# Slot numbers carried in a node's row, and adjacency degrees split between the table and the blocks, in a four-layer graph kernel

## The chip, the cores and the metric

The kernel runs on one core of a Trainium2 chip. The metric is the device time of one execution in microseconds, as the median of several. The record marks each execution as fast or slow by its time and clock; all that are told of here are fast. Engines are called as in the profile: PE (matmuls), PEld (weight loads, beside PE), DVE, ACT, POOL, SP.

## The reference, cut to what matters

Four layers, each `x = layernorm(x + layer(x, adj))`, with x of 8 x 2048 x 64 and a dense 2048 x 2048 adjacency `adj`. Only the first layer is touched. It mixes each node with its hyperedges (64 of them, mask `H` of 2048 x 64, 1 to 12 a node):

```python
h = x @ W
alpha = softmax(where(H.T > 0, leaky_relu(h @ a_node), NEG))        # over nodes
agg = einsum('ben,bnf->bef', alpha, h)                              # one row a hyperedge: the "table"
beta = sigmoid((h @ a_gn)[:, None, :] + (agg @ a_ge)[:, :, None])
all_he = elu(beta * h + (1 - beta) * agg)                           # per node and hyperedge: the "blocks"
coefs1 = softmax(where(H > 0, attn(elu(agg)), NEG))                 # over a node's hyperedges
g = einsum('bne,benf->bnf', coefs1, all_he)
deg = maximum(adj.sum(-1), 1)
industry = einsum('nm,bmf->bnf', adj / deg, x @ W_ind)              # the "products"
```

## The kernel before

Nodes are sorted by their number of hyperedges (`order`). A row tile is 128 sorted nodes; it needs as many blocks as its fullest node has hyperedges: 12, 5, 5, 4, 4, 4, 3, 3, 3, 3, 2, 2, 2, 2, 2, 1, together 57. Block s of a tile takes each node's s-th hyperedge. A **slot number** (0, or 1 to 12) says for each pair of hyperedge and node which block that is. A **one-hot** is the 128 x 128 matrix `slot == s + 1`; a matmul with it picks table rows.

Before, the rows of H are gathered in sorted order, and the slot numbers of all 2048 nodes lie ready in one resident tile `slot` before the first block:

```python
for t in range(NT):
    nc.gpsimd.indirect_dma_start(out=hs[:, t, :], in_=h_ne, in_offset=...order[:, t:t + 1]...)
...
for c in range(NCH):      # masks, transposes, cumulative count
    ...
    nc.vector.tensor_tensor(slot[:, cols(c)], pcm, mt, ALU.mult)
```

The block stage interleaves blocks with the product matmuls, which `fill(n)` hands out:

```python
def begin(t):
    hrow = pl.tile([P, BF + 8], F32, tag="hrow", bufs=2)
    nc.gpsimd.indirect_dma_start(out=hrow, in_=hs_hbm[:], ...order[:, t:t + 1]...)    # row fetch
    S = sum(n > t for n in SLOT_TILES)
    both = split(pb, hrow[:, 0:BF], "hr", 2, [P, BF])
    for s in range(S):
        o = pl.tile([P, P], F32R, tag="o", bufs=17)
        nc.gpsimd.tensor_scalar(o, slot[:, cols(t, P)], float(s + 1), None, op0=ALU.is_equal)
        mm(ps[:, s]..., lhsT=o, rhs=ts2, start=True, stop=True)                       # one-hot sums
    ...                                                                               # R, co on DVE
now = begin(0)
for t in range(NT):
    S, both, ohs, R, co = now
    for s in range(S):
        for i, (l, r) in enumerate(((ident_r, both[0]), (ident_r, both[1]), (ohs[s], tab2))):
            mm(pz, lhsT=l, rhs=r, start=i == 0, stop=i == 2)
        if s == 0 and t + 1 < NT:
            fill(3)
            now = begin(t + 1)
        fill(8)
        ...                                 # pz *= R (DVE), y = exp (ACT), elu and * co (DVE)
        nc.gpsimd.tensor_tensor(acc, acc, y, ALU.add)
```

Each engine runs its instructions in the order that the scheduler gave it. Products work on x split into a high half (a cast on ACT) and a low half (a subtraction, here on DVE).

## Time and profile before

The median of three runs is 2227.4 us (2225.26 to 2234.32). From the profiled execution:

| point of the first layer | us |
|---|---|
| first row fetch for the blocks | 101.31 |
| first product matmul | 112.2 |
| last product matmul ends | 292.84 |
| first gather of the next layer | 297.5 |
| span | 2227.2 |

Read it as two stages: up to 112 us the table and the adjacency, bound by loads; from there the blocks, bound by PE. The views are in the prediction. This is the timeline (start, length, engine, line, operation, count of instructions; in brackets the engine's idle time before it and what ended it; `...` marks lines left out):

```profile
163.59 1.24 POOL L623 TENSOR_SCALAR o<-slot 128x128 fp32r<-128x128 bf16 x2
166.66 0.53 POOL L623 TENSOR_SCALAR o<-slot 128x128 fp32r<-128x128 bf16 x1 [1.83 <-PE pz L171]
...
172.18 0.51 PE L171 MATMUL ps<-ts,o 128*128 128x16 f32 x4
```

POOL makes one-hots in small groups between other work and, in this view, is held only by `pz`, that is, by an old one-hot's buffer that a block still reads. When PE comes to the sums it does four in 0.51 us.

### The profile page before, as it was taken

The numbers are of one execution on the slowest core, as the hardware profiler recorded it, in microseconds if no ns is written. First come the engines' busy times: TensorE is split into PE (matmuls) and PEld (weight loads), VectorE is DVE, ScalarE is ACT, GpSimd is POOL, SyncE is SP. The second block draws the span as 40 slices with busy tenths as digits, with TensorE's granted clock in tenths as the row PEclk, the third lists the DMA queues.
The fourth block names the chain that finished last, engine by engine and source line by source line (L and its number), as shares of the span: only waits on it lengthen the run. The fifth ranks groups of instructions, "written<-read, shape, count | busy, mean of one in ns | idle before, by whom it ended". The sixth has DMA issues, their size and how long they took to land.

```text
span 2227.2 us, 19810 instructions
## 1 busy us (share of the span) xinstructions
PE 1993.1 (89%) x7318; PEld 1289.3 (58%) x7318; DVE 1139.1 (51%) x1900; ACT 338.3 (15%) x584; POOL 551.0 (25%) x499
## 2 busy tenths in 40 slices
PE   7799978888759999799999999999986989999994
PEld 4488745555644444375456456447434777777873
DVE  5479956666532222216864773782784344331312
ACT  1322323222111111010010001001000011111110
POOL 5457466564323323200110110110010001010202
PEclk7889989999969999999999999999998999999997
DMA  8723334322210000000000000000001223200000
GB/s 263 237 66 91 95 91 107 83 70 63 76 46 0 19 19 19 19 24 5 10 5 3 10 8 1 10 8 3 8 8 32 76 72 85 62 19 1 20 1 21
DMA packets 99306, 103.26 MB, mean 46 GB/s; under 512 B 63088, under 2 KB 63136, under 8 KB 99008
## 3 DMA queue, kind: packets, MB, share of 16 engines
q1 hardware_dynamic: 73248, 83.09, 12.8%
q0 software_dynamic: 4064, 9.10, 1.7%
q10 hardware_dynamic: 21888, 9.70, 1.6%
q8 instruction: 60, 0.98, 0.2%
q14 instruction: 46, 0.38, 0.1%
HBM read 75.59 MB, written 26.28 MB: 46 GB/s over the span
## 4 chain that ended last, share of the span: by engine, by line
PE 63%; DVE 12%; DMA 12%; POOL 7%; issue 4%; ACT 2%; SPq 0%; ACTq 0%; POOLq 0%; DVEq 0%
PE py L967 18%; PE u L171 17%; PE u L914 10%; PE u L527 9%; DMA fcav<-in_adj_t 7%; POOL ln_r L155 3%; PE pz L171 2%; DVE fcav L1061 2%; PE pf L171 1%; PE pr L171 1%; DMA x<-x_hbm 1%; DVE ln_v L151 1%; DVE ln_c L145 1%; DVE ln_m L143 1%; ACT r L149 1%
## 5 line engine op out<-in xcount | busy, mean ns | idle before, releaser
L967 PE MATMUL py<-wp,xg 128*128 128x512 f32 x1024 | 448.5, 597 | 8.5 <-DVE fcav L972 5.8
L967 PEld LDWEIGHTS py<-wp,xg 128*128 128x128 f32 x1024 | 193.6, 191 | 254.4 <-issue 216.4
L171 PE MATMUL u<-adj,hi 128*128 128x512 f32 x768 | 256.5, 415 | 0.0
L171 PE MATMUL u<-adj,lo 128*128 128x512 f32 x768 | 246.5, 400 | 1.1 <-DVE lo L1026 1.1
L914 PE MATMUL u<-pt,xn 128*128 128x512 f32 x512 | 227.5, 603 | 8.3 <-DVE u L923 7.1
L972 DVE TENSOR_TENSOR fcav<-py,emb_n 128x512 f32<-128x512 f32 x256 | 177.0, 691 | 52.0 <-PE py L967 37.5
L975 POOL TENSOR_TENSOR r<-r,bias 128x256 f32<-128x256 f32 x32 | 23.3, 729 | 636.0 <-DVE r L973 636.0
L973 DVE TENSOR_REDUCE r<-fcav 128x32 f32<-128x512 f32 x256 | 175.4, 685 | 8.1
L914 PEld LDWEIGHTS u<-pt,xn 128*128 128x128 f32 x512 | 97.3, 193 | 130.2 <-issue 114.7
L527 PE MATMUL u<-adj,vh 128*128 128x512 f32 x512 | 158.3, 408 | 15.4 <-ACT vh L166 11.6
L171 PEld LDWEIGHTS u<-adj,hi 128*128 128x128 f32 x768 | 143.2, 190 | 40.8 <-issue 11.5
L171 PEld LDWEIGHTS u<-adj,lo 128*128 128x128 f32 x768 | 144.6, 190 | 35.4 <-DVE lo L1026 1.6
L527 PE MATMUL u<-adj,vl 128*128 128x512 f32 x512 | 152.1, 398 | 0.0
L155 POOL TENSOR_TENSOR ln_r<-ln_e,neg_half 128x8 f32<-128x8 f32 x64 | 106.1, 1658 | 174.9 <-DVE ln_e L153 166.9
L908 DVE TENSOR_SCALAR pt<-pt 128x512 f32<-128x512 f32 x64 | 49.1, 784 | 172.8 <-ACT pt L907 171.3
L1045 POOL TENSOR_TENSOR r<-r,xn 128x512 f32<-128x512 f32 x16 | 20.4, 1275 | 418.9 <-DVE r L1044 418.9
L527 PEld LDWEIGHTS u<-adj,vh 128*128 128x128 f32 x512 | 96.2, 189 | 45.7 <-ACT vh L166 13.1
L912 POOL TENSOR_TENSOR acc<-acc,pt 128x512 f32<-128x512 f32 x60 | 79.6, 1327 | 162.6 <-DVE pt L908 159.8
L527 PEld LDWEIGHTS u<-adj,vl 128*128 128x128 f32 x512 | 96.4, 189 | 22.1 <-issue 0.7
L1061 DVE SCALAR_TENSOR_TENSOR fcav<-fcav,adj 128x512 f32<-128x512 f32 x64 | 44.5, 695 | 117.6 <-DMA fcav<-in_adj_t 117.1
L149 ACT ACTIVATE r<-ln_c 128x512 f32<-128x512 f32 x64 | 40.4, 631 | 288.4 <-DVE ln_c L145 274.8
L709 POOL DMA_INDIRECT gn<-gs_hbm,rank x64 | 69.7, 1088 | 34.7 <-issue 14.2
(316 smaller groups left out, 2774.3 us busy)
## 6 DMA issues: line engine op xcount, KB each, us to landing
a<-in_adj_t SPq DMA_DIRECT2D x32, 512.0 KB, 5.9
fcav<-in_adj_t SPq DMA_DIRECT2D x64, 256.0 KB, 2.8
x_hbm<-r SPq DMA_DIRECT2D x20, 256.0 KB, 2.3
hs_hbm<-st ACTq DMA_DIRECT2D x16, 260.0 KB, 5.4
xt<-in_x_t SPq DMA_DIRECT2D x16, 256.0 KB, 5.4
u_hbm<-ut SPq DMA_DIRECT2D x16, 256.0 KB, 2.7
gs_hbm<-acc SPq DMA_DIRECT2D x16, 256.0 KB, 2.0
ut<-u_hbm SPq DMA_DIRECT2D x16, 256.0 KB, 3.2
```

What stands on the lines that cost most here:

```text
L149: nc.scalar.activation(r, xc, AF.Square)
L155: nc.gpsimd.tensor_tensor(rstd, vare, neg_half[:, :groups], ALU.pow)
L171: tc.keep_in_program_order(nc.tensor.matmul(*args, **kw))
L527: nc.tensor.matmul(u[c], lhsT=half[:, j, :], rhs=adj[t][:, cols(c)], start=t == 0 and i == 0, stop=ends and not own,)
L709: nc.gpsimd.indirect_dma_start(out=gn[:, j, :], out_offset=None, in_=g_rows, in_offset=bass.IndirectOffsetOnAxis(ap=rank4[:, p, c * JT + j ...
L908: nc.vector.tensor_scalar(pt, pt, 1.0, None, op0=ALU.max)
L912: nc.gpsimd.tensor_tensor(acc, acc, pt, ALU.add)
L914: nc.tensor.matmul(u[p], lhsT=xn[p][:, t, :], rhs=pt, start=t == 0, stop=t == NT - 1)
L967: nc.tensor.matmul(py.rearrange("p o d -> p (o d)"), lhsT=xg[b][:, q, cols(j, P)], rhs=wp[:, q, cols(k)], start=q == 0, stop=q == 1,)
L972: nc.vector.tensor_tensor(pr, py, e_b, ALU.mult)
L973: nc.vector.tensor_reduce(r[:, j, b, cols(k, OH)], pr, AX.X, ALU.add)
L1061: nc.vector.scalar_tensor_tensor(a, a, 1.0, adj[t][:, cols(k)].bitcast(F32), op0=ALU.mult, op1=ALU.not_equal, accum_out=left[:, t, k:k + 1],)
```

## The change

Its intent: the 16 gathers of H rows go. Slot numbers are made in natural node order, before `order` is known, and written into the row of each node in HBM, so that the row fetch brings them along. Four of the 16 adjacency tiles, and the degree sums over them, move behind the first row fetch, into the block stage, so that the blocks can begin earlier. Cut to its core:

```diff
-    slot = hy.tile([P, N], BF16, name="slot")
+    HROW = BF + 8 + 2 * E
+    hs_hbm = dram.tile([N, HROW], F32, name="hs_hbm")
...
+        for t in range(NT):
+            nc.tensor.matmul(pcm[:, t, :], lhsT=mt[:, cols(t, P)], rhs=tri_e, start=True, stop=True)
+        nc.vector.tensor_tensor(slot, pcm, m_n, ALU.mult)
+        for i in range(2):
+            queued(nc.sync.dma_start(hs_hbm[:, k:k + E]..., slot))
...
-            st = pa.tile([P, BF + 8], F32, tag="st", name="st", bufs=2)
+            st = pa.tile([P, BF + 8], F32, tag="st", name="st", bufs=3)
...
-                part[c] = split(pb, xc.pop((p, c)), f"v{c}", 1, [P, JT, P])
+                part[c] = split(pb, xc.pop((p, c)), f"v{c}", 1, [P, JT, P], nc.gpsimd)
...
+        def load_adj_end(t):
+            for c in range(NCH):
+                a = pb.tile([P, JT, P], F32, tag="x", name="a", bufs=XB)...
+                nc.sync.dma_start(a, adj_t[t * P:(t + 1) * P, cols(c)])
+                tc.keep_in_program_order(nc.gpsimd.tensor_copy(adj[t][:, cols(c)], a))
...
         def begin(t):
+            fetch_rows(t + 1)
+            hrow = hrows.pop(t)
             S = sum(n > t for n in SLOT_TILES)
+            pt = pps.tile([P, P], F32, tag="mm", name="pslot", bufs=3)
+            transpose(pt, hrow[:, BF + 8:])
+            slot = pl.tile([P, P], BF16, tag="slot", name="slot", bufs=2)
+            nc.scalar.copy(slot, pt)
...
-                nc.gpsimd.tensor_scalar(o, slot[:, cols(t, P)], float(s + 1), None, op0=ALU.is_equal)
+                tc.keep_in_program_order(
+                    nc.gpsimd.tensor_scalar(o, slot, float(s + 1), None, op0=ALU.is_equal)
+                )
...
+        fetch_rows(0)
+        fetch_rows(1)
+        load_adj_end(NT - 4)
+        load_adj_end(NT - 3)
         now = begin(0)
+        load_adj_end(NT - 2)
+        load_adj_end(NT - 1)
...
-                fill(8)
+                fill(7)
```

More of the change, by code (lines that the diff above doesn't have):

```diff
@@ L63, in tile_gnn_fast @@
     adj_t: bass.AP,
-    h_ne: bass.AP,
+    h_en: bass.AP,
+    h_nt: bass.AP,
     w0: bass.AP,
@@ L88, in tile_gnn_fast @@
     B, N, F = x.shape
-    E = h_ne.shape[1]
+    E = h_en.shape[0]
     D = emb.shape[1]
@@ L160, in grouped, with split @@
         return a.rearrange("p t (b f) -> p (t b) f", f=F)
-    def split(pool, src, tag, bufs, shape):
+    def split(pool, src, tag, bufs, shape, eng=nc.vector):
         hi = pool.tile(shape, F32R, tag=f"{tag}h", name=f"{tag}h", bufs=bufs)
@@ L166, in split @@
         nc.scalar.copy(hi, src)
-        nc.vector.tensor_tensor(lo, src, hi, ALU.subtract)
+        eng.tensor_tensor(lo, src, hi.bitcast(F32) if eng is nc.gpsimd else hi, ALU.subtract)
         return hi, lo
@@ L201, in tile_gnn_fast @@
     order = hy.tile([P, NT], U32, name="order")
-    slot = hy.tile([P, N], BF16, name="slot")
     inv_row = hy.tile([P, N], F32, name="inv_row")
-    tri2 = hy.tile([P, P], BF16, name="tri2")
-    nc.vector.memset(tri2, 0.0)
-    make_upper_triangular(nc, tri2[0:E, 0:E], 1.0, diag=True)
-    nc.vector.tensor_copy(tri2[E:P, E:P], tri2[0:E, 0:E])
-    hs_hbm = dram.tile([N, BF + 8], F32, name="hs_hbm")
+    HROW = BF + 8 + 2 * E
+    hs_hbm = dram.tile([N, HROW], F32, name="hs_hbm")
     x1_hbm = [dram.tile([P, NT, P], F32, name=f"x1_hbm{p}") for p in range(NP)]
@@ L219, in tile_gnn_fast @@
     adj = [adj_pool.tile([P, N], F32R, name=f"adj{t}") for t in range(NT - XT)]
+    ph_scope = ExitStack()
+    pph = ph_scope.enter_context(tc.tile_pool(name="ph", bufs=1, space=PSUM))
     with tc.tile_pool(name="pa", bufs=1) as pa, tc.tile_pool(name="pa_ps", bufs=1, space=PSUM) as pps:
@@ L227, in tile_gnn_fast @@
         m_n = pa.tile([P, NT, E], F32, name="m_n")
-        nc.sync.dma_start(m_n, h_ne.rearrange("(t p) e -> p t e", p=P))
+        nc.sync.dma_start(m_n, h_nt)
+        m_en = pa.tile([E, N], F32, name="m_en")
+        nc.scalar.dma_start(m_en, h_en)
         xt = [xs.tile([P, NP, P], F32, name=f"xt{t}") for t in range(NT)]
@@ L242, in tile_gnn_fast, with queued @@
             nc.scalar.dma_start(bd66[b * F:(b + 1) * F, b, 0:F], w0)
+        def queued(dma):
+            tc.keep_in_program_order(dma)
         def load_adj(t):
@@ L248, in load_adj @@
                 a = pa.tile([P, HN], F32, tag="a", name="a", bufs=4)
-                nc.sync.dma_start(a, adj_t[t * P:(t + 1) * P, cols(k, HN)])
-                if t < NT - XT:
-                    nc.gpsimd.tensor_copy(adj[t][:, cols(k, HN)], a)
-                else:
-                    nc.scalar.copy(adj[t][:, cols(k, HN)], a)
-        for t in range(NT - XT):
+                queued(nc.sync.dma_start(a, adj_t[t * P:(t + 1) * P, cols(k, HN)]))
+                nc.gpsimd.tensor_copy(adj[t][:, cols(k, HN)], a)
+        for t in range(4):
             load_adj(t)
@@ L314, in tile_gnn_fast @@
         nc.vector.tensor_scalar(wrong[:, 1:2], pc[:, 0:1], float(N), None, op0=ALU.is_lt)
+        tri_e = pa.tile([E, E], BF16, name="tri_e")
+        make_upper_triangular(nc, tri_e, 1.0, diag=True)
+        mt = pa.tile([E, N], BF16, name="mt")
+        nc.vector.tensor_scalar(mt, m_en, 0.0, None, op0=ALU.is_gt)
+        pcm = pph.tile([P, 2, C], F32, tag="ph", name="pcm", bufs=2)
+        pcm = pcm.rearrange("p k (t e) -> p (k t) e", e=E)
+        for t in range(NT):
+            nc.tensor.matmul(pcm[:, t, :], lhsT=mt[:, cols(t, P)], rhs=tri_e, start=True, stop=True)
+        slot = pa.tile([P, NT, E], F32, name="slot")
+        nc.vector.tensor_tensor(slot, pcm, m_n, ALU.mult)
+        for i in range(2):
+            k = BF + 8 + i * E
+            queued(nc.sync.dma_start(hs_hbm[:, k:k + E].rearrange("(t p) e -> p t e", p=P), slot))
+        for t in range(4, NT - XT):
+            load_adj(t)
         tl = pa.tile([P, NT], F32, name="tl")
@@ L346, in tile_gnn_fast @@
         nc.vector.scalar_tensor_tensor(order, po[:, 0, :], float(P), olo, op0=ALU.mult, op1=ALU.add)
-        hs = pa.tile([P, NT, E], F32, name="hs")
-        for t in range(NT):
-            nc.gpsimd.indirect_dma_start(
-                out=hs[:, t, :], out_offset=None, in_=h_ne,
-                in_offset=bass.IndirectOffsetOnAxis(ap=order[:, t:t + 1], axis=0),
-            )
         for dst, v in ((fcb_col, fc_b), (av_col, av)):
@@ L374, in tile_gnn_fast @@
         for t in range(NT):
-            ph = pps.tile([P, 2, C], F32, tag="ph", name="ph", bufs=2)
+            ph = pph.tile([P, 2, C], F32, tag="ph", name="ph", bufs=2)
             for p in range(NP):
@@ L402, in tile_gnn_fast @@
             )
-            nc.scalar.dma_start(hs_hbm[t * P:(t + 1) * P, :], st)
+            nc.scalar.dma_start(hs_hbm[t * P:(t + 1) * P, 0:BF + 8], st)
             for k in range(2):
@@ L414, in tile_gnn_fast, with degrees @@
         adj_end = ctx.enter_context(tc.tile_pool(name="adj_end", bufs=1, side="right"))
-        for t in range(NT - XT, NT):
-            adj.append(adj_end.tile([P, N], F32R, name=f"adj{t}"))
-            load_adj(t)
-        du = [pps.tile([P, 2, C], F32, tag="ph", name=f"du{g}", bufs=2) for g in range(2)]
-        ones_r = pa.tile([P, P], F32R, name="ones_r")
+        adj += [adj_end.tile([P, N], F32R, name=f"adj{t}") for t in range(NT - XT, NT)]
+        ones_r = hy.tile([P, P], F32R, name="ones_r")
         nc.gpsimd.tensor_copy(ones_r, ones)
-        def degrees(first, end):
-            for t in range(first, end):
+        du = [pph.tile([P, 2, C], F32, tag="ph", name=f"du{g}", bufs=2) for g in range(2)]
+        def degrees():
+            for t in range(NT):
                 for c in range(NCH):
@@ L430, in degrees, with some_degrees @@
                     )
-        degrees(0, 8)
-        for c in range(NCH):
-            m2 = pa.tile([P, JT, 2, E], F32, tag="m2", name="m2", bufs=2)
-            for i in range(2):
-                nc.vector.tensor_scalar(m2[:, :, i, :], hs[:, c * JT:(c + 1) * JT, :], 0.0, None, op0=ALU.is_gt)
-            pt = pps.tile([P, C], F32, tag="sm", name="pt", bufs=2)
-            for j in range(JT):
-                nc.tensor.transpose(pt[:, cols(j, P)], m2[:, j].rearrange("p i e -> p (i e)"), ident)
-            mt = pa.tile([P, C], BF16, tag="mt", name="mt", bufs=2)
-            nc.scalar.copy(mt, pt)
-            pcm = pps.tile([P, C], F32, tag="sm", name="pcm", bufs=2)
-            nc.tensor.matmul(pcm, lhsT=tri2, rhs=mt, start=True, stop=True)
-            nc.vector.tensor_tensor(slot[:, cols(c)], pcm, mt, ALU.mult)
+                    yield
+        degree_passes = degrees()
+        def some_degrees(tiles):
+            for _ in range(tiles * NCH):
+                next(degree_passes)
+        some_degrees(6)
         gv = pagg[:, :, 0:G * (F + 1)].rearrange("p k (g c) -> p k g c", c=F + 1)
@@ L458, in tile_gnn_fast @@
         )
-        tab = pa.tile([E, B, F], F32, tag="st", name="tab", bufs=2)
+        tab = pa.tile([E, B, F], F32, tag="st", name="tab", bufs=3)
         tsm = pa.tile([E, 2, B], F32, name="tsm")
@@ L480, in tile_gnn_fast @@
             ))
-        degrees(8, 10)
+        some_degrees(2)
         het = pa.tile([P, NP, E], F32, name="het")
@@ L488, in tile_gnn_fast @@
             nc.scalar.activation(tf[:, b], pf, AF.Tanh, bias=fcb_col)
-        degrees(10, NT - XT)
+        some_degrees(2)
         pse = pps.tile([E, B], F32, tag="sm", name="pse", bufs=2)
@@ L493, in tile_gnn_fast @@
                 mm(pse[:, 2 * p + b:2 * p + b + 1], lhsT=tf[:, b, p, :], rhs=av_col, start=True, stop=True)
-        degrees(NT - XT, NT)
         nc.vector.tensor_scalar(sc[:, 1, :], pse, CLIP, -CLIP, op0=ALU.min, op1=ALU.max)
@@ L503, in tile_gnn_fast @@
         nc.vector.tensor_tensor(ts2[E:P, :], tsf, ts2[0:E, :], ALU.subtract)
-        for g in range(2):
-            nc.scalar.copy(inv_row[:, cols(g, 2 * C)], du[g].rearrange("p k c -> p (k c)"))
     def load_x(dst, p, c):
@@ L542, in tile_gnn_fast @@
         pps = pb_scope.enter_context(tc.tile_pool(name="pb_ps", bufs=1, space=PSUM))
+        XB = 5
         def products():
@@ L547, in fetch @@
             def fetch(p, c):
-                xc[p, c] = pb.tile([P, JT, P], F32, tag="x", name="xc", bufs=4)
+                xc[p, c] = pb.tile([P, JT, P], F32, tag="x", name="xc", bufs=XB)
                 load_x(xc[p, c], p, c)
@@ L553, in parts @@
             def parts(p, c):
-                part[c] = split(pb, xc.pop((p, c)), f"v{c}", 1, [P, JT, P])
+                part[c] = split(pb, xc.pop((p, c)), f"v{c}", 1, [P, JT, P], nc.gpsimd)
             for c in range(NCH):
                 fetch(0, c)
+            yield from degree_passes
             for c in range(NCH):
                 parts(0, c)
+            for g in range(2):
+                nc.scalar.copy(inv_row[:, cols(g, 2 * C)], du[g].rearrange("p k c -> p (k c)"))
             deg1 = pb.tile([P, NT], F32, name="deg1")
@@ L563, in products @@
                     own = (2 * g, 2 * g + 1)
-                    u = {c: pps.tile([P, C], F32, tag=f"u{c}", name=f"u{c}", bufs=1) for c in own}
+                    ug = pph.tile([P, 2, C], F32, tag="ph", name="ug", bufs=2)
+                    u = {c: ug[:, c % 2, :] for c in own}
                     for t in range(NT):
@@ L600, in products @@
                         nc.sync.dma_start(u0_hbm[p][:, cols(c)], ut)
+        def load_adj_end(t):
+            for c in range(NCH):
+                a = pb.tile([P, JT, P], F32, tag="x", name="a", bufs=XB).rearrange("p t f -> p (t f)")
+                nc.sync.dma_start(a, adj_t[t * P:(t + 1) * P, cols(c)])
+                tc.keep_in_program_order(nc.gpsimd.tensor_copy(adj[t][:, cols(c)], a))
         filler = products()
@@ L608, in tile_gnn_fast, with fetch_rows @@
         pl = pb_scope.enter_context(tc.tile_pool(name="pl", bufs=1))
-        def begin(t):
-            hrow = pl.tile([P, BF + 8], F32, tag="hrow", name="hrow", bufs=2)
-            nc.gpsimd.indirect_dma_start(
-                out=hrow, out_offset=None, in_=hs_hbm[:],
-                in_offset=bass.IndirectOffsetOnAxis(ap=order[:, t:t + 1], axis=0),
-            )
+        hrows = {}
+        def fetch_rows(t):
+            if t < NT and t not in hrows:
+                hrows[t] = pl.tile([P, HROW], F32, tag="hrow", name="hrow", bufs=3)
+                tc.keep_in_program_order(nc.gpsimd.indirect_dma_start(
+                    out=hrows[t], out_offset=None, in_=hs_hbm[:],
+                    in_offset=bass.IndirectOffsetOnAxis(ap=order[:, t:t + 1], axis=0),
+                ))
+        def begin(t):
+            fetch_rows(t + 1)
+            hrow = hrows.pop(t)
             S = sum(n > t for n in SLOT_TILES)
+            pt = pps.tile([P, P], F32, tag="mm", name="pslot", bufs=3)
+            transpose(pt, hrow[:, BF + 8:])
+            slot = pl.tile([P, P], BF16, tag="slot", name="slot", bufs=2)
+            nc.scalar.copy(slot, pt)
             both = split(pb, hrow[:, 0:BF], "hr", 2, [P, BF])
@@ L667, in tile_gnn_fast @@
             pass
+    ph_scope.close()
     hy_scope.close()
@@ L1772 @@
 FAST = (
-    "x", "x_t", "adj_t", "h_ne", "w0", "w_ind", "a_node", "a_gn", "a_ge", "fc_w", "fc_b", "av", "w1_t",
-    "emb", "emb_t", "w_pool", "b_pool", "iv", "w31_t", "b31", "w32_t", "w32", "b32", "w0_t",
+    "x", "x_t", "adj_t", "h_en", "h_nt", "w0", "w_ind", "a_node", "a_gn", "a_ge", "fc_w", "fc_b", "av",
+    "w1_t", "emb", "emb_t", "w_pool", "b_pool", "iv", "w31_t", "b31", "w32_t", "w32", "b32", "w0_t",
 )
@@ L1803 @@
         "x_t": xt,
+        "h_nt": a["L0_gnn_H"].reshape(N // 128, 128, -1).transpose(1, 0, 2),
         "w32": a["L3_gnn_W2"],
```

## The prediction

> **What bounds the kernel now.** I read the page first: PE is busy 89% of 2227.2 us, but that mixes stages. The change touches only the first layer, so I asked for the chain of waits from 0 to 112 us, then for busy times by stretch, then for groups of instructions and the timeline. The chain, with what carries it (start, length, what):
>
> ```profile
> 52.26 5.42 DMA hs<-in_h_ne,order
> ...
> 64.77 7.27 DMA hs_hbm<-st
> ...
> 78.88 7.67 PE du L171 x32
> ...
> 94.40 4.22 DMA a<-in_adj_t
> 98.62 0.02 issue
> 98.65 1.04 ACT adj L253
> 99.69 0.92 ACT inv_row L505
> 100.61 0.70 issue
> 101.31 6.49 DMA hrow<-hs_hbm,order
> ```
>
> The reader should see three parts. A loop makes the node rows `st` and stores them; it is held by gathers of hyperedge rows (52 us) and by the landing of its own stores, with two buffers (65 us). Then comes the hyperedge table, with degree sums (du) between its steps. Then the last adjacency tiles land, and only at 101.31 us is the first row fetch for the blocks issued. The stretches (length, then busy time and count of PE, PEld, DVE, ACT, POOL, then granted clock, DMA share, GB/s):
>
> ```profile
> 40.00:60.00 20.00, 13.34 (x65) 8.77 (x65) 10.17 (x28) 2.29 (x10) 17.75 (x18) 0.83 0.88 276
> 60.00:80.00 20.00, 15.22 (x60) 9.07 (x61) 15.01 (x35) 3.24 (x12) 12.29 (x12) 0.75 0.92 323
> ...
> 112.00:140.00 28.00, 27.47 (x112) 22.35 (x112) 14.72 (x31) 5.30 (x10) 13.57 (x14) 0.71 0.27 62
> 140.00:190.00 50.00, 50.00 (x227) 41.09 (x227) 46.94 (x82) 15.44 (x27) 36.45 (x36) 1.00 0.22 64
> 190.00:240.00 50.00, 50.00 (x228) 41.31 (x227) 49.65 (x97) 16.45 (x28) 35.29 (x36) 1.00 0.37 106
> 240.00:264.00 24.00, 20.45 (x91) 16.00 (x89) 23.96 (x44) 7.47 (x13) 9.56 (x8) 1.00 0.27 89
> ```
>
> So the table stage is bound by DMA (about 0.9 share), with POOL nearly full from 40 to 60 us. The block stage, from about 112 to 293 us, is bound by PE with DVE close behind; only at 240 to 264 us does DVE hold PE (PE 20.45 of 24). What fills POOL and DVE:
>
> ```profile
> L251 POOL CAST adj<-a 128x1024 fp32r<-128x1024 f32 x24 | 25.2, 1054 | 24.8 <-DMA a<-in_adj_t 24.7
> L350 POOL DMA_INDIRECT hs<-in_h_ne,order x16 | 15.4, 965 | 8.0 <-DVE order L346 4.8 <-issue 3.2
> ...
> L664 POOL TENSOR_TENSOR acc<-acc,y 128x512 f32<-128x512 f32 x41 | 56.6, 1381 | 52.5 <-DVE y L663 36.3 <-DVE R L627 11.7 <-issue 4.1
> L623 POOL TENSOR_SCALAR o<-slot 128x128 fp32r<-128x128 bf16 x57 | 37.5, 665 | 11.4 <-PE pz L171 9.9
> ```
>
> **What the Trainium skill says.** "DMA: Bandwidth & Descriptors", Specifications: about 358 GB/s of HBM per core, and transfers below 512 B fall short of line rate. The trace's mean is 276 to 323 GB/s in the stretches above; 4 us slices reach 378 to 389, so the measurement is above the page's limit at moments. The new slot columns are written in pieces of 256 B; I charge them like the old 2048-piece load of the hyperedge matrix, which landed in 4.4 us. "SBUF — State Buffer", Who interferes with whom: a DVE instruction with two SBUF inputs and a GpSimd instruction that reads SBUF exclude each other for the whole instruction. The trace agrees: the low-half subtractions of the x chunks take 0.67 us undisturbed and 1.40 us at worst, and an 8-element tensor_scalar on DVE means 0.82 us. "TensorE: Matmul & The Clock Gate", What's actually happening: the clock is halved after idling and comes back after some 3.4 us of work. Here the granted clock is 0.50 from 104 to 120 us and again 0.55 to 0.59 from 124 to 132 us, after the 4.6 us of tiny degree transposes; a 512-column matmul then starts every 0.43 us, not every 0.229 (8 in 1.83 us).
>
> **The change, part by part.**
> 1. Gathers gone. 16 gathers (15.4 us of POOL), 8 mask instructions on DVE (4.4 us busy, 9.9 us of waiting for the gathers), 16 transposes and four PSUM copies go. In their place: one mask over 64x2048 (estimate 1.4 us, from 0.76 us for 128x1024), 16 small matmuls (about 2 us), one 128x1024 multiply (about 1.2 us), two slot writes of 0.5 MB. The order of instructions shows them before the first node tile, so the loop starts some 5 us later, at about 15 us, but `order` is ready earlier than its 31.4 us of before, because fewer things lie between.
> 2. Three `st` buffers, not two. A store lands in about 5 to 7 us under load, and a tile takes about 1.9 us from first write to the store's issue. Two buffers give (1.9+5.5)/2 = 3.7 us a tile, as seen (10 tiles from 38 to 75.8 us); three give about 2.8. From tile 3 at about 27 us that ends the loop at 27+12x2.8 = 61 us, where it was 75.8. PE's last sums follow at once; before they waited for the last mask transposes until 78.9.
> 3. The table: 78.88 to 93.6 us before = 14.7 us; two degree tiles fewer stand before its transposes, so 12.8 us: ready near 75 us.
> 4. Twelve adjacency tiles, not sixteen, before the blocks: 12.6 MB + x 4.2 + rows 4.3 + masks and slots 2.1 = 23.2 MB. At 300 to 320 GB/s that is 73 to 77 us. So table and DMA meet: first fetch at about **77 us**, where it was 101.3.
> 5. The start of the blocks gets dearer, and this takes most of the gain. POOL's order is: two fetches, 8 half-size casts of late adjacency tiles, 12 one-hots, 8 more casts, a fetch, 5 one-hots, then four low halves of x, which moved from DVE. The first five late pieces land about 3 us after 77; the casts (0.53 us each, half of 1.05) go on to 85; the 12 one-hots (7.04 us before) to 92; the second 8 casts wait for their DMA until about 97.5; fetch and five one-hots to 102. PE does its first block at 93 us but stands at the one-hot sums of row tile 1 until 102. Then 24 degree matmuls and three blocks, half of it at the half clock, about 9 us: the products begin at about **111.5 us**. Before, they began at 112.2. PE by then has four blocks behind it instead of one.
> 6. The rest is PE's. Left at 111.5 us: 512 product matmuls + 53x3 block matmuls = 671x0.229 = 153.6 us; 40 one-hot sums x 0.12 = 4.8; tiny transposes 4.6; 16 inverse transposes and 14 of the new slot transposes, about 3.6. Sum 166.6, plus about 4 for the half clock after the tiny transposes and about 3 of gaps. End 285 us; before 292.9.
> 7. The low halves of x (14.2 us) leave DVE for POOL, at about 1.3 us each (an addition of that size takes 1.29): 21 us. This removes most of the DVE hold at 240 to 264 us (3.5 us of PE), which is in the 3 us of gaps above. Seven product matmuls a block instead of eight leave a tail of 536-(57x7+15x3) = 92 of them after the last block, 21 us of pure PE; harmless if PE was the bound before it.
> Everything after the first layer is the same on every engine. The sum: 292.9-285 = 8 us, rounded up to 9 because the table may be ready earlier: **2218 us**.
>
> **Rivals.** (a) The whole 24 us of the earlier fetch is kept, if the casts and one-hots overlap better than POOL's order suggests: about 2203 us. Against it stands POOL's fixed order and PE's wait at tile 1. (b) POOL becomes the bound in the blocks: a row tile of five slots would cost it 1.3 (fetch) + 3.0 (one-hots) + 5.4 (four additions) + 2.6 (two low halves) = 12.3 us, against 12.9 of PE (53x0.229+0.7); DVE, which excludes POOL, could push this over. PE would stand in the blocks and the 21 us tail would not help: 2225 to 2235 us. POOL's 36.45 of 50 us before leaves room for it, so I give this a quarter. (c) The loop does not speed up, because the adjacency loads, no longer held by POOL, lengthen the stores' landing to 7 us or more: fetch at 82 us, 2223 us.
>
> **Range and chances.** Between (a) and (b), with 3 us for run-to-run scatter (2225.26 to 2234.32 in three runs): 2206 to 2230. Two per cent is 44.5 us; no path here has that, since only 24 us are even in play: faster 0.02, within 2% 0.97, slower 0.01.
>
> **What would show it.** In the changed kernel's profile: the first row fetch near 77 us (steps 1 to 4); POOL's casts ahead of and after the 12 one-hots, and PE idle between its first block and the one-hots of tile 1 (step 5); first product matmul near 111 us; PE full from there, DVE with gaps, and a run of about 92 product matmuls ending near 285 us (6 and 7). The prediction is wrong if the first product starts before 100 us, if PE has idle stretches in the blocks that end with POOL, or if the later layers differ by more than a few us.

## More of the kernel before

Over the whole stage, from 112 to 293 us, no wait of PE ends with a one-hot (busy time, mean ns of one, idle time before and what ended it):

```profile
L623 POOL TENSOR_SCALAR o<-slot 128x128 fp32r<-128x128 bf16 x43 | 30.0, 702 | 10.6 <-PE pz L171 9.9
...
L171 PE MATMUL ps<-ts,o 128*128 128x16 f32 x45 | 6.4, 240 | 2.4 <-DVE co L636 2.4
```

## The result, and the profile after

The changed kernel took **2327.82 us** in the median of four runs (2324.58 to 2331.87), where the kernel before took 2230.70 in its four. The ratio is 1.0438, with a 95% interval of 1.0406 to 1.0471: slower. Here and below, a ratio is the mean time of one kernel's fast runs over that of the other's of the same rounds, so it is not quite the ratio of the medians. One per cent is about 22 us.

| point of the first layer, us | before | after |
|---|---|---|
| first row fetch for the blocks | 101.31 | 81.62 |
| first product matmul | 112.2 | 119.86 |
| last product matmul ends | 292.84 | 389.75 |
| first gather of the next layer | 297.5 | 394.55 |
| span | 2227.2 | 2322.8 |

The 97 us are there at the first gather of the next layer, and the spans differ by 95.6; so all of the loss lies between 82 and 390 us. A caution for what follows: the changed kernel and seventeen of the experiments have the same program up to the first row fetch, and their profiled executions put it anywhere from 75.4 to 83.8 us. So a start-up time of a single execution is good to some us only. The start-up, in the timeline:

```profile
81.62 1.05 POOL L627 DMA_INDIRECT hrow<-hs_hbm,order  x1 [2.23 <-issue]
...
92.41 7.03 POOL L647 TENSOR_SCALAR o<-slot 128x128 fp32r<-128x128 bf16 x12
...
99.50 2.85 POOL L612 CAST adj<-a 128x512 fp32r<-128x512 f32 x5
...
106.94 3.25 POOL L647 TENSOR_SCALAR o<-slot 128x128 fp32r<-128x128 bf16 x5
...
119.86 0.74 PE L172 MATMUL ug<-adj,v0h 128*128 128x512 f32 x2
```

POOL's order is the predicted one, and the fetch is 20 us earlier than before, but the products begin 8 us later than before. Now the stretches that the prediction showed for the kernel before (length, then busy time and count of PE, PEld, DVE, ACT, POOL, then granted clock, DMA share, GB/s):

```profile
40.00:60.00 20.00, 17.24 (x100) 11.65 (x99) 13.17 (x38) 2.75 (x14) 5.21 (x5) 1.00 0.96 289
60.00:80.00 20.00, 16.93 (x89) 12.17 (x88) 12.33 (x25) 3.69 (x12) 11.71 (x11) 1.00 0.85 308
...
140.00:190.00 50.00, 38.17 (x148) 30.32 (x147) 30.30 (x52) 12.17 (x22) 24.22 (x24) 0.83 0.18 50
190.00:240.00 50.00, 34.45 (x120) 26.86 (x119) 28.64 (x57) 9.21 (x17) 23.16 (x25) 0.78 0.20 63
240.00:264.00 24.00, 19.27 (x74) 15.27 (x73) 13.39 (x24) 6.55 (x12) 12.09 (x12) 0.82 0.22 58
```

Up to 80 us things are better than before: PE has more done and POOL is freed of the gathers. In the blocks every engine does less in the same time, PE too, and its clock has fallen. No engine is full: this is a stage bound by waits. How much is waiting and how much is the clock, the same view shows when it is asked for the whole stage, first of the kernel before, then after:

```profile
112.00:293.00 181.00, 176.92 (x775) 144.16 (x774) 162.91 (x311) 51.62 (x89) 103.57 (x99) 0.95 0.28 82
```

```profile
120.00:390.00 270.00, 206.21 (x773) 162.49 (x773) 145.18 (x280) 54.09 (x100) 109.45 (x106) 0.83 0.17 52
```

PE does nearly the same number of matmuls. Before, it is idle for 181.00 - 176.92 = 4.1 us; after, for 270.00 - 206.21 = 63.8. That is 59.7 us more of idle time. The same work is busy for 206.21 - 176.92 = 29.3 us longer, at a clock of 0.83 instead of 0.95. With the 8 us of later start this makes 97.

What PE waits for, one boundary between two row tiles shows:

```profile
148.60 0.27 PE L175 MATMUL pslot<-ident,hrow 128*128 128x128 f32 x1
148.91 0.27 ACT L640 CAST slot<-pslot 128x128 bf16<-128x128 f32 x1 [1.18 <-PE pslot L175]
...
150.35 1.27 POOL L695 TENSOR_TENSOR acc<-acc,y 128x512 f32<-128x512 f32 x1 [2.49 <-DVE y L694]
...
151.78 1.06 POOL L627 DMA_INDIRECT hrow<-hs_hbm,order  x1 [0.16 <-issue]
...
152.88 2.77 POOL L647 TENSOR_SCALAR o<-slot 128x128 fp32r<-128x128 bf16 x5
153.50 1.37 PE L172 MATMUL ps<-ts,o 128*128 128x16 f32 x3 [4.63 <-POOL o L647]
...
156.94 1.05 PE L172 MATMUL ug<-adj,v0h 128*128 128x512 f32 x2
```

PE transposes the slot columns of the fetched row; ACT copies them. The one-hots then have their place on POOL behind the last addition of the tile before, which waits for DVE, and behind a row fetch. PE stands for 4.63 us, then gets one-hots at POOL's pace, one in about 0.6 us, and afterwards matmuls of 512 columns start every 0.43 us (156.94 to 157.79 for two) until about 159.5. After the start there are 14 more boundaries, and each has such a wait, 2.39 to 6.07 us long, 59.5 us together: as much as the added idle time. With each of the 14 the clock falls too, even with the five that are shorter than 3 us: the one of 2.39 us ends at 267.29 us, and from 269 to 272 us the granted clock is 0.50. The groups of instructions from 112 to 366 us say the same in sum (busy time, mean ns of one, idle time before and what ended it):

```profile
L647 POOL TENSOR_SCALAR o<-slot 128x128 fp32r<-128x128 bf16 x40 | 21.3, 559 | 0.8
...
L172 PE MATMUL ps<-ts,o 128*128 128x16 f32 x40 | 14.2, 354 | 63.5 <-POOL o L647 61.7
```

Each one-hot is even quicker than before (559 ns, against 702 from 112 to 293 us in the kernel before). It is only late: 61.7 us of PE's idle time end with one.

The Trainium skill bears on both parts. "PSUM — Partial Sum Buffer", Engine vs sequencer instructions: "ScalarE/VectorE/GpSimdE queues are strict FIFO", and matmuls keep their order on TensorE. The boundary agrees: for 4.63 us nothing on PE passes the waiting sums, though the products behind them then run without a wait of their own. And the clock page that the prediction cites has the clock halved after idling: 0.43 us instead of 0.229 after a wait of 4.63 us agrees.

### The profile page after: what moved, and what is told of

Read it like the earlier page. It is cut to its first block, busy times and chain, and to the rows that moved or that the text cites. A ratio compares the mean times of both kernels' runs of the same rounds, so it can differ in the third digit from the quotient of the medians.

```text
span 2322.8 us, 19833 instructions
## 1 busy us (share of the span) xinstructions
PE 2019.2 (87%) x7330; PEld 1307.4 (56%) x7330; DVE 1126.3 (48%) x1872; ACT 333.3 (14%) x588; POOL 561.6 (24%) x515
## 4 chain that ended last, share of the span: by engine, by line
PE 53%; DVE 10%; DMA 9%; POOL 6%; issue 4%; ACT 2%; SPq 0%; POOLq 0%; ACTq 0%; DVEq 0%
PE py L999 17%; PE u L172 11%; PE u L946 10%; PE u L527 9%; DMA fcav<-in_adj_t 6%; POOL ln_r L156 3%; DVE fcav L1093 1%; POOL gn L741 1%; PE ug L172 1%; DVE ln_c L146 1%; DVE ln_v L152 1%; PE pr L172 1%; DVE ln_m L144 1%; DMA x<-x_hbm 1%; PE pf L172 1%
## 5 line engine op out<-in xcount | busy, mean ns | idle before, releaser
L527 PE MATMUL u<-adj,vh 128*128 128x512 f32 x512 | 158.7, 409 | 15.2 <-ACT vh L167 11.4
L172 PE MATMUL ps<-ts,o 128*128 128x16 f32 x57 | 20.7, 362 | 76.2 <-POOL o L647 73.9
```

The costliest lines, as they stand in the source:

```text
L172: tc.keep_in_program_order(nc.tensor.matmul(*args, **kw))
L527: nc.tensor.matmul(u[c], lhsT=half[:, j, :], rhs=adj[t][:, cols(c)], start=t == 0 and i == 0, stop=ends and not own,)
```

## The experiments

Eighteen kernels ran; all were correct. **Theory A**: PE stands because the one-hots are late, since their input now comes with the row. A1 puts the lateness on the slot row itself (transpose and copy), A2 on the one-hots' place in POOL's order. **B**: POOL has too much to do, with the low halves. **C**: the tail of products behind the blocks is what was lost. The runs, with ratios to the kernel before of the same rounds (e1 and e3 to e7 had two executions each, the others four to six):

| run | median us | ratio, 95% interval |
|---|---|---|
| e1, slot row a tile ahead | 2313.16 | 1.0370, 1.0326 to 1.0414 |
| e5, one-hots in free order | 2295.37 | 1.0290, 1.0231 to 1.0350 |
| e7, e1 and e5 together | 2252.98 | 1.0110, 1.0054 to 1.0165 |
| e6, products between one-hots and sums | 2306.04 | 1.0348, 1.0295 to 1.0401 |
| e2, slot row and one-hots a tile ahead | 2242.79 | 1.0057, 1.0022 to 1.0093 |
| e3, low halves on DVE | 2333.52 | 1.0461, 1.0412 to 1.0511 |
| e4, eight products a block | 2331.12 | 1.0460, 1.0413 to 1.0508 |
| e8, e2 with tile 1 before the last casts | 2243.36 | 1.0076, 1.0051 to 1.0102 |
| e9, e2 with eight products | 2247.52 | 1.0095, 1.0068 to 1.0121 |
| e10, e9 with late casts on ACT | 2245.18 | 1.0081, 1.0054 to 1.0107 |
| e13, e8 with one-hots spread | 2272.79 | 1.0198, 1.0162 to 1.0233 |
| e12, e8 with three y buffers | 2244.84 | 1.0077, 1.0042 to 1.0113 |
| e11, e8 with low halves on DVE | 2233.33 | 1.0015, 0.9980 to 1.0050 |
| e15, before with low halves on POOL | 2239.10 | 1.0049, 1.0014 to 1.0084 |
| e19, e8 with all x loads on SP | 2236.67 | 1.0020, 0.9997 to 1.0042 |
| e16, e11 with another start | 2231.40 | 1.0011, 0.9990 to 1.0032 |
| e17, e16 with eight products | 2227.42 | 1.0002, 0.9976 to 1.0029 |
| e18, e17 with all degrees first | 2231.37 | 0.9998, 0.9972 to 1.0023 |

### Are the one-hots late, and why?

**e1**: the transpose and copy of the slot row a tile earlier, and the row fetch with them; the one-hots stay.

```diff
                     now = begin(t + 1)
+                    prep(t + 2)      # row fetch, transpose, copy to slot (3 buffers)
```

> The changed kernel with each row tile's slot transpose and its copy issued one tile earlier; the row fetch that begin() issued now comes behind the one-hots instead of ahead of them; the one-hots and their sums stay where they are. Theory A1 (the slot, made by PE only just before its use, is what PE waits for): the wait of PE for POOL one-hots (73.9 us) falls below 20 us and the time to about 2240 to 2260 us. Theory A2 (the slot is early enough, but POOL's queue holds the last addition of the tile before and a 1.06 us row fetch ahead of the one-hots): only the fetch goes from the path, about 1.2 us x 14 tiles, so 2305 to 2320 us. Rival B (POOL has too much work in the blocks, from the low halves of x): no change, 2320 to 2335 us.

2313.16 us; PE still waits 51.8 us for one-hots (61.7 in the changed kernel). Moving the input ahead helps little: as A2 has it, not A1.

**e5**: the input stays late, but the one-hots are not held in program order on POOL.

```diff
-                tc.keep_in_program_order(
-                    nc.gpsimd.tensor_scalar(o, slot, float(s + 1), None, op0=ALU.is_equal)
-                )
+                nc.gpsimd.tensor_scalar(o, slot, float(s + 1), None, op0=ALU.is_equal)
```

> The changed kernel with the one-hots no longer held in program order on POOL, so that the scheduler may put them ahead of additions and of the fetch; the slot is still made just before. Theory A2: one-hots start as soon as the slot is there (about 0.6 us after the transpose instead of 4.0), some 2.5 to 3.5 us a tile over 14 tiles plus less half clock: 2260 to 2290 us. Theory A1: PE still waits for the slot, no more than 10 us gained, 2315 us or more. Rival B: unchanged, 2320 to 2335 us.

2295.37 us, a wait of 36.7 us: a third of the loss, less than A2 alone expected. The late input is a second link: in this run one-hots wait 21.1 us for the copy of the slot row.

**e7**: both edits together.

> The slot rows transposed and copied one tile earlier, and the one-hots not held in program order on POOL, so both halves of the chain are loosened at once, but no one-hot is asked for early in the program. Theory A: the two parts add up and the scheduler may make one-hots early, since their input is there; 2240 to 2262 us, near the kernel with one-hots a tile ahead. If the two runs that loosened one half each had hit the same time by some third cause: about 2295.

2252.98 us, as expected. No wait of PE for one-hots of 1 us or more is left in its trace (one of 13.2 us, for a row fetch, is new). Alone, the two edits bring 0.7 and 1.5 points; together 3.3. While either link is late the other counts for little.

**e6**: the block's seven products put between the one-hots' issue and their sums.

```diff
+            if t:
+                fill(7)
+            for s, o in enumerate(ohs):
                 mm(ps[:, s]..., lhsT=o, rhs=ts2, start=True, stop=True)
...
-                fill(7)
+                else:
+                    fill(7)
```

> The changed kernel, with the seven product matmuls of the block put between the issue of the one-hots and the sums that use them, so that PE has 7 x 0.229 = 1.6 us of other work in each of the 15 waits. Theory A (PE stands for the one-hots because they are made late): the wait shrinks by about 1.6 us a row tile, 24 us, and a little clock comes back; 2290 to 2305 us. If the waits in the trace are only a symptom of some other bound of the blocks: 2320 to 2330.

2306.04 us, 1 us above the range; the wait shrinks by 17.9 us to 43.8. So the waits are true loss: PE's other work, put into them, comes off the time.

**e2**: slot row and one-hots a tile ahead (and the row fetch, as in e1), the sums in their old place.

```diff
+        def prep(t):                         # for tile t + 2, in the first block of tile t
+            fetch_rows(t + 1)
+            ...transpose, copy to slots[t]
+            for s in range(sum(n > t for n in SLOT_TILES)):
+                o = pl.tile([P, P], F32R, tag="o", name="o", bufs=17)
+                tc.keep_in_program_order(nc.gpsimd.tensor_scalar(o, slots[t], float(s + 1), ...))
+                ready[t].append(o)
```

> The changed kernel with slot transpose, copy and one-hots of a row tile all issued one tile earlier; only the sums stay at the old place. Theory A (A1 and A2 together: the serial chain transpose, copy, queue of POOL, one-hots, sums at each tile): PE's wait for one-hots all but vanishes (below 12 us, most of it at the start), the products end at 285 to 295 us, the time is 2215 to 2235 us. Rival B: the same instructions on POOL, so at most 15 us gained, 2310 us or more. Rival C (seven products a block leave 92 products as a tail): that tail stays, so 2300 us or more.

2242.79 us: 3.8 of the 4.4 points, 85 of the 98 us. In PE's waits from 112 to 305 us (total, times, longest) what was 61.7 us is now

```profile
PE ps L172 <- POOL o L646: 2.3, 2, 1.9
```

Theory A holds. But it is 8 us above the expected range and still slower than the kernel before: something else is lost.

**e3**: the changed kernel with the low halves of x back on DVE, for rival B.

```diff
-                part[c] = split(pb, xc.pop((p, c)), f"v{c}", 1, [P, JT, P], nc.gpsimd)
+                part[c] = split(pb, xc.pop((p, c)), f"v{c}", 1, [P, JT, P])
```

> The changed kernel with the low halves of x back on DVE, nothing else. Rival B (POOL's load): the wait for one-hots falls by half or more and the time by 40 us or more, to 2285 us or less. Theory A: POOL idles most of the blocks already (109 us busy of 250), so 2315 to 2335 us, with the wait of PE for one-hots still above 60 us.

2333.52 us: nothing comes back. POOL's load does not hold these blocks.

**e4**: `fill(8)` instead of `fill(7)`, for rival C.

> The changed kernel with eight product matmuls a block again instead of seven, nothing else: the tail of products shrinks from 99 to about 42. Theory A: the waits for one-hots are at the row tiles, not at the products, so the end moves by a few us at most; 2315 to 2335 us. Rival C (the product tail after the blocks is what was lost): up to 13 us come back from 57 products, about 2310.

2331.12 us; no gain. The products end at 389.7 us, as they did with the longer tail.

### What the remaining 13 to 18 us are

**e8** (one-hots of tile 1 before the last casts), **e9** (eight products a block) and **e10** (that, and the late casts on ACT) change the start and the tail of e2:

```diff
         now = begin(0)
+        prep(1)
         load_adj_end(NT - 2)
         load_adj_end(NT - 1)
-        prep(1)
```

> Slot row and one-hots one tile ahead, and those of row tile 1 now before the second eight casts on POOL instead of after them. Theory: the run with one-hots ahead still stood 4.5 + 4.9 us for one-hots at the start, and started its products at 120 us against 112 before; of this about 5 us come back: 2233 to 2242 us. If the start does not set the end of the blocks (DVE does): no change, 2240 to 2246.

> Slot row and one-hots one tile ahead, with eight product matmuls a block: the tail after the blocks, 22 us of PE alone with DVE at 8 of 20, is cut to about 9 us, and products fill PE where DVE holds it. If DVE holds the blocks at 180 to 240 us and the tail is work that could have run there: 2230 to 2238 us. If PE was full where it counts: 2240 to 2246.

> As the one with one-hots ahead and eight products a block, and the last 16 half-size adjacency casts on ACT instead of POOL, with the one-hots of row tiles 0 and 1 made before them. POOL is then free for fetches and one-hots from the first fetch on. If the start-up queue of POOL is the rest of the loss: products start near 110 us and the time is 2215 to 2230, at or below the kernel before. If the DMA of the late tiles sets the start: 2230 to 2238.

2243.36, 2247.52 and 2245.18 us: none is faster. e8 lies in the range given for no change; e9 and e10 lie above both of theirs. In e8's profiled execution, its fastest, the first product starts at 112.3 us, as in the kernel before, but the last one still starts at 299.1 (304.4 in e2, whose products start at 120.1). So the start is not all that sets the end, though a part of it may carry through; a shorter tail gains nothing here. In e10 the late tiles' casts had got behind a slot copy in ACT's queue, and the DMA share from 90 to 100 us was 0.03; the products began at 119.2. In e8's timeline of the blocks this stands out:

```profile
164.48 2.82 POOL L646 TENSOR_SCALAR o<-slot 128x128 fp32r<-128x128 bf16 x4
...
167.38 1.29 POOL L168 TENSOR_TENSOR v2l<-xc,v2h 128x512 fp32r<-128x512 f32 x1
...
168.70 0.47 ACTq L511 DMA_DIRECT2D xc<-in_x  x1
169.21 0.60 ACT L698 ACTIVATE y<-pz 128x512 f32<-128x512 f32 x1 [5.08 <-POOL v2l L168]
...
170.68 0.47 PE L172 MATMUL pz<-hrh,ident_r 128*128 128x512 f32 x1 [1.57 <-DVE y L700]
```

ACT stands for 5.08 us before an exponential and is let go by a low half on POOL, which the exponential does not read; DVE and then PE stand behind it. (The exponential's own input is ready only near 166.9 us, when DVE has made it, so some 2.3 of the 5.08 us are this wait alone.) I took it for a buffer of `y` that POOL's late additions keep (theory Q), and DVE's load for the rival (theory D).

**e13**: one-hots spread, one made in each block, instead of two to five at once.

```diff
                     nc.gpsimd.tensor_tensor(acc, acc, y, ALU.add)
+                onehots(t + 2, s, 12 if s == S - 1 else s + 1)
```

> Slot row one tile ahead and the one-hots of the tile after next made one in each block instead of two to five at once. Theory Q: POOL's bursts vanish and the additions come in time; 2228 to 2236 us, the table's earlier end is then partly a gain against the 2243. Theory D: 2240 to 2246.

2272.79 us, far outside both. The one-hots of a tile are now spread over the blocks of one that has hardly more blocks, each behind an addition, and they come late again: PE's waits for them are 30.4 us. The edit brought back the first loss, so it says nothing of Q or D.

**e12**: three buffers `y`, paid for with four x chunks instead of five.

> One-hots a tile ahead, those of row tile 1 before the last casts, and three buffers y instead of two (the place is taken from the x chunks, four instead of five), so that ACT need not wait for POOL's addition so soon. Theory Q: 2230 to 2238 us. Theory D: no change, 2240 to 2246. If four x chunks come late: slower, with waits on the loads of x.

2244.84 us: no change. ACT's waits for POOL's additions (8.5 us in seven in e8) are gone from its list, and the same 5.1 us wait for POOL's low half is there. So theory Q in this form gets no support. It is not a clean test, because the edit also takes away an x chunk, and that could cost what the third `y` brings.

**e11**: low halves on DVE (the edit of e3), on e8.

> One-hots a tile ahead, those of row tile 1 before the last casts (the run of 2243), and the low halves of x back on DVE, which is the third place of POOL's queue in the blocks. Theory Q (what is left of the loss is POOL's queue: a burst of one-hots and a low half of 1.29 us ahead of an addition keep a buffer y from coming free, ACT stands up to 5 us for it, then DVE, then PE): the burst stays but gets shorter, 2232 to 2239 us. Theory D (DVE bounds the blocks, it has only 1 us of 20 to spare at 180 to 240 us): 14 us more on DVE cost, 2246 to 2256.

2233.33 us against e12's 2244.84 in the same rounds. Fourteen us more on DVE make the kernel faster, so D falls as it was put; the low halves on POOL cost 0.6 points, some 12 to 14 us (by the medians and by the ratios). With the one-hots late (e3) that was hidden.

**e15**: the kernel before, with this one part of the change.

> The kernel before with one part of the change alone: the low halves of the x chunks on POOL instead of DVE. My prediction's step 7 says that this removes the DVE hold at 240 to 264 us, 3.5 us: 2224 to 2228 us. Theory Q: the low halves stand ahead of additions in POOL's queue and hold y, so nothing is gained or some us are lost: 2230 to 2238.

2239.10 us, 0.5 per cent or 11 us slower: the low halves cost this by themselves. The trace shows where DVE's relief went. It is rid of 14.2 us of low halves, but its instructions that read two operands from SBUF (the core's main on-chip memory) take longer beside a busier POOL: 41 `y<-y,co` 891 ns each instead of 744, 16 `acc<-y,co` 924 instead of 698, 16 `hrl` 943 instead of 860, together 11.2 us more. `pz<-pz,R`, which reads one operand from PSUM (the matmuls' accumulator), stays at 687 ns (685 before). That is the exclusion that the prediction cites, at work against its step 7. It would explain why little is gained, not why 11 us are lost.

**e19**: since the `y` buffers were not it, I looked at what ACT's queue holds just ahead of the late exponential. It is a load of x, at 168.70 us, the moment that POOL's low half is done with its chunk. Half of the loads of x are issued by ACT. In e19, SP issues them all.

```diff
-            eng = nc.sync if b == 0 else nc.scalar
+            eng = nc.sync
```

> The run of 2243 (one-hots ahead, those of row tile 1 before the last casts, low halves on POOL) with all loads of x chunks issued by SP; there half of them are issued by ACT. Theory X: a low half that POOL makes late keeps its x chunk, the next load into that buffer waits for it in ACT's own queue, and ACT's exponentials stand behind that load (5.1 us at 164 to 169 us, ended by POOL's low half); with the loads on SP they no longer do, and most of the 13 us that low halves on DVE bring come back: 2231 to 2237 us. If low halves cost through POOL's load or its exclusion with DVE instead: 2241 to 2246.

2236.67 us, a ratio of 1.0020 against e8's 1.0076; the intervals do not overlap. ACT's waits for POOL's low halves (8.8 us in two waits in e8) are gone from its list. This speaks for theory X: a load's wait for its buffer is served in the issuing engine's queue. The Trainium skill says so in its account of a DMA that GpSimd issues ("DMA: Bandwidth & Descriptors", Anatomy of one DMA — SWDGE (gpsimd) path: a semaphore wait of a DMA is done by the issuing sequencer before dispatch); here the load is one that ACT issues, and it starts at 168.70 us, just before the exponential that stood. It is not fully settled. The profiled executions of e8 and e19 start their last products at 299.1 and 299.4 us, and e8's profiled one was the fastest of its four; counted from each one's first row fetch (77.2 and 82.6 us) e19 is 5 us quicker, from the first product 2. The same line of code also loads x in the next layer, so e19 moved those loads too; but from the first gather of that layer on, e8 takes 1931.8 us and e19 1931.1, so nothing shows there. And in e15 no exponential waits for a low half: theory X does not explain that loss.

### Where the earlier fetch went

**e16**, **e17** and **e18** tried to beat both kernels: e11 with the 16 late casts on ACT and both one-hot groups before the first block; with eight products a block; and with all casts and degree sums before the first block.

```diff
-                tc.keep_in_program_order(nc.gpsimd.tensor_copy(adj[t][:, cols(c)], a))
+                tc.keep_in_program_order(nc.scalar.copy(adj[t][:, cols(c)], a))
...
+        prep(0, nc.vector.tensor_copy)       # e18
+        prep(1, nc.vector.tensor_copy)
+        for t in range(NT - 4, NT):
+            load_adj_end(t)
+        fill(6 * NCH)
         now = begin(0)
```

> A version meant to beat both: one-hots a tile ahead and low halves on DVE (the run of 2233, whose products start at 116 us), and in the start-up the 16 half-size adjacency casts on ACT, which stands idle there, in their old place in the program, with both one-hot groups issued before the first block. POOL then has only fetches and one-hots from 82 us on. If POOL's queue holds the late tiles' loads (in the run of 2233 the DMA share is 0.43 at 90 to 100 us, since the five buffers wait for casts): products start near 104 us and all ends some 8 to 12 us earlier; 2220 to 2226 us. If DVE holds the blocks whenever they start: 2230 to 2236.

> The same with eight product matmuls a block instead of seven. In the run of 2233 the blocks end at 282 us and PE is then alone with products until 297. If DVE holds the blocks, products put into them are free and the tail gets shorter: 2 to 6 us below the same with seven. If PE and DVE share the hold: no change within 3 us.

> The last candidate to beat both. From the run of 2227 (one-hots ahead, low halves on DVE, casts on ACT, eight products a block): there ACT's queue still stood 5.6 us for the first block before it cast the last adjacency pieces (99.2 us), and the products started at 113.7. Here all 16 casts and all degree sums come before the first block, and the first two slot rows are copied by DVE so that the one-hots do not wait for ACT. If the order of the start-up queue is what swallows the earlier fetch: last cast near 98 us, products from about 103 us, 2216 to 2223 us. If DVE holds the blocks whenever they start, the first block now being later: 2226 to 2232.

2231.40, 2227.42 and 2231.37 us: all equal to the kernel before. e16 and e18 lie in the ranges given for "DVE holds the blocks whenever they start"; e17's median is 4 us below e16's, as that reading had it, but the intervals of the two overlap, so this is not shown. Not even e18, with its free queues, starts the products at 103 us:

```profile
81.32 17.74 SPq L611 DMA_DIRECT2D a<-in_adj_t  x16
...
104.72 0.62 ACT L612 CAST adj<-a 128x512 fp32r<-128x512 f32 x1 [0.17 <-DMA a<-in_adj_t]
...
110.31 1.22 PE L172 MATMUL ug<-adj,v0h 128*128 128x512 f32 x2 [0.29 <-ACT inv_row L564]
```

The late tiles are issued from 81.32 us on, through five buffers; the last is cast at 104.72 us and the first product runs at 110.31. In the kernel before, the last tile was cast by 99.69. Products need all 16 tiles, because their accumulators take over the space of the degree sums. Moving four tiles behind the fetch made the blocks earlier, but not what the products wait for. From there on PE and DVE are both full (in e18, DVE is busy 19.7 to 19.9 of every 20 us from 180 to 260), so I take it that three blocks done ahead buy next to nothing; no run tests this by itself.

## Why the prediction was wrong

- **Steps 1 to 4** held in kind. The stores of the loop are issued from 24.4 to 66.1 us, 15 steps of 2.8 us as predicted (before: 14.8 to 76.9, 4.1 each; the same loop takes 2.5 to 2.9 in the experiments' traces that I looked at). But the first comes 10 us later than before, not 5. The fetch is at 81.62 and not 77, but with 75.4 to 83.8 us from one execution to another 77 is not refuted.
- **Step 5** held in its order. Its mis-sized term is the first group of casts: put at an end of 85 us, it ended at 92.4. Of these 7.4 us, 4.6 are the later fetch, the rest are pieces that landed late; the one-hots took 7.03 us as predicted. The products began at 119.86, not 111.5. The reading that the start takes most of the gain was right: e16 to e18 get no gain out of it.
- **Step 6, "The rest is PE's", is the step that failed.** It summed PE's work as if nothing but PE could hold it, with about 4 us for the half clock after the tiny transposes and 3 of gaps. In their place came 63.8 us of idle PE and 29.3 us more of busy time for nearly the same matmuls, at the lower clock. The cause is the late one-hots: with them made a tile ahead (e2), 85 of 98 us are gone. The prediction saw PE stand for the one-hots of row tile 1 in its step 5, and booked it as start-up; the same chain comes at each of the 14 later boundaries, with 59.5 us of waits. The data were there: before, `slot` was resident, and POOL's 57 one-hots had almost only buffer waits ahead of them (9.9 of 11.4 us). The change's third word, "carried", takes away that lead.
- **Step 7** had the wrong sign. It made the low halves on POOL a gain of up to 3.5 us; on the kernel before they cost 11 (e15): it charged POOL with them, and not DVE's other instructions, which grew by 11.2 us. (Its reading of the exclusion was also off: the low halves on DVE reach 1.79 us at worst, not 1.40, and the 8-element instruction that it adds has one SBUF operand, not two.) That PE was full did not make the tail of 92 products the trouble either: e4 and e9 show no gain with a shorter one.
- **Rival (b)** put a quarter on POOL as the bound, by its load, at 2225 to 2235. The load was not it (e3; POOL was busy for 109.45 of 270 us). What held was POOL's order, and no rival had that. The range also left out a part of its own rivals (2203 us of (a) and all of (b) above 2230), and "slower", which came, had a chance of 0.01.
- The last paragraph named the sign that would refute it, "idle stretches in the blocks that end with POOL". That is what came.

Not settled: how the low halves cost 11 to 14 us in detail (with the one-hots ahead, e19 speaks for the loads in ACT's queue, but only by its times; in e15 that wait is not seen), and what the rest of 3 us in e11 is, if it is anything.

## What to carry to other kernels

When data that was resident comes to be loaded in pieces, ask what was made from it ahead of time, and count the chain from the piece's arrival to its use once for each piece, not once for the start. An in-order queue is read by what stands ahead of the instruction, not by its load: POOL was 40% busy and cost 85 us. And look at which engine issues a load: in e8 the arithmetic of ACT seems to have stood behind one that waited for its buffer.

## What the Trainium skill lacked or had wrong

- "DMA: Bandwidth & Descriptors", Specifications: its limit of about 358 GB/s of HBM per core is not borne out with one core at work. The changed kernel shows slices of about 1 us at 417 to 422 GB/s between 20 and 62 us, and the kernel before 4 us slices at 378 to 389. Further down, the same page has 408.7 GB/s for a single core's load stream, which fits these better than its own table does.
- The same page says where a DMA's semaphore wait is done, but not what can follow for the engine's arithmetic: in e8 ACT stood 5.08 us up to such a load, and with the loads on SP the ratio was 1.0020 instead of 1.0076.
- "TensorE: Matmul & The Clock Gate", HAM oscillation — how this bites in real kernels: it does treat waits that recur, but gives as its rule that PE must have no gaps above some 3.4 us. Here five waits of 2.39 to 2.91 us, each with only a few small sums right after it, were also each followed by 2 to 3 us at a granted clock of 0.50. Over all 14, 59.5 us of waits came with 29.3 us more of busy time, half as much again.
- I found no page that speaks of one-hots or other operands made ahead of their use on an in-order queue; here the lead was worth 85 us.
